# A layer norm's reciprocal deviation moved from GpSimd to ScalarE, with normalising and some partial sums one slot earlier

## The chip, the cores and the metric

The kernel runs on one core of one Trainium2 chip. The metric is the device time of one execution in microseconds (us), the median of three runs. All data are float32. A core has five engines that matter here: TensorE (PE in the profile; PEld is its weight load), VectorE (DVE), ScalarE (ACT), GpSimd (POOL) and SyncE (SP), which starts the transfers.

## The reference

Two layers work on x of shape (2, 256, 256, 128), each as x + f(group_norm(x)). The first is an attention along one image axis. The second, where the change lies, is a selective state-space scan:

```python
xz = x @ in_proj_w.T                      # 128 -> 2 x 256 channels
xi, z = jnp.split(xz, 2, axis=-1)
xi = silu(depthwise_conv3x3(xi) + conv_b)
xs = xi.reshape(B, 256, L)                # L = 256*256 positions in order
dts, Bs, Cs = split(x_proj_w @ xs)        # 8 + 16 + 16 rows
delta = softplus(dt_w @ dts + dt_b)
h = exp(delta*A) * h + (delta*xs) * Bs    # step by step along L, 16 states a channel
y = sum(h * Cs over states) + Ds * xs
mu = y.mean(-1); var = ((y - mu)**2).mean(-1)
y = (y - mu) * rsqrt(var + 1e-5) * ln_g + ln_b     # over the 256 channels
out = (y * silu(z)) @ out_proj_w.T
```

The change concerns the rsqrt in the layer norm, and the moments at which its result is used.

## The kernel before

The first part (lines up to about 560) makes weights and group statistics and runs the attention; it takes some 2670 us. The second part is one software pipeline over 128 **steps**. A step is four image rows of one image, T = 1024 positions. The 256 channels times 16 states are cut into **units** of 128 partitions: 32 channels times 4 states. So a step has 32 units; `unit(t)` splits slot number t into step k, channel half h, state group m and quarter q. The loop at the end of the kernel runs over **slots** t, one unit to a slot. Slots are counted here within their step, 0 to 31. Slot 0 of a step is the one in which its first unit is scanned.

What a unit goes through, each by one function:

- `decay` (L947, ScalarE): da = exp(a * delta), one slot ahead of the scan.
- `drive` (L957, GpSimd): hb = du * B for a pair of units, three slots ahead.
- `scan` (L969, VectorE): h = da*h + hb along the 1024 positions.
- `product` (L983, VectorE): yc = h * C. For the five pairs in `POOLED` (units 2-3, 6-7, 10-11, 18-19, 26-27) GpSimd makes it instead, as a pair, in `products` (L992). Both write into a pool with four yc buffers, each for a pair of units.
- `remember` (L974, ScalarE): keeps the last column of h as the next step's start. It is the last thing ScalarE does in a slot, so ScalarE follows VectorE slot by slot.
- `add_up` (L1014, TensorE): 16 matmuls that sum four units' yc over the states into the accumulator y. It is written at the end of slot u + 6 for the four units from u on, so in slots 2, 6, 10, ..., 30. A yc buffer is free only after it. With four buffers, the product of unit u + 8 needs those of u, and so waits for the sum of slot u + 6. For a group that opens a channel half it is preceded by `d_diag` (L1007), which starts y with Ds * xs.
- `y_out` (L1027, ScalarE): y to SBUF after the last sum of a half, in slots 4 and 20.

Two other strands are laid into the same slots by a table written by hand (`at(t, piece)`):

- `project` works about two steps ahead: `turn` and `normalise` (L652, L657), `conv` (L670; nine taps for each of four pieces, in slots 3 to 6, 11 to 14, 19 to 22 and 27 to 30), `conv_out` (L681), `gate` (L695, with `gate_out` L706), `states` (L718, L731), `size` (L736) with `size_out` (L747). All of these share one PSUM bank (`ps_p`, one buffer): the next matmul of this strand starts only when ScalarE has evacuated the one before. Silu and softplus (L689, L711, L755) follow, one big ScalarE operation each. [...] each has an ACT_TABLE_LOAD of its own, and the next exp (L947) has one to come back.
- `finish` works one step behind, on one row at a time. A row starts in slots 0, 8, 16 and 24. Its pieces and their offsets from there: `turn` 0 (L819, TensorE transposes and centres y), `stats` 1 (L831, ScalarE squares and sums), `scales` 2 (L838 and L839, GpSimd: variance, then power -0.5), `norm` 4 (L843, ScalarE), `back` 5 (L854, TensorE), `gated` 6 (L862, VectorE), `mix` 7 (L866, L870, TensorE: output sums), `leave` 8 (L880, ScalarE: to SBUF and out).

Within a slot the order is fixed: drive and products, decay, scan and product, `y_out`, then the pieces of the table with those of `finish` ahead of those of `project` and those that run on TensorE last, then `add_up`, then `remember`. Each engine takes its instructions in exactly that order.

Of the kernel before, what the change touches and what calls it, by code (L numbers as in the profile page):

```python
# [15 lines left out]
P = 128  # L16
# [5 lines left out]
def attn_then_ssm_kernel(  # L22
# [59 lines left out]
    make_identity(nc, ident)  # L82
    ones_mean = const0.tile([P, P], F32, name="ones_mean")
    nc.vector.memset(ones_mean, 1.0 / P)
    neg_half = const.tile([P, TB // P], F32, name="neg_half")
    nc.vector.memset(neg_half, -0.5)

# [188 lines left out]
    with ExitStack() as actx:  # L276
# [51 lines left out]
        def project(n, tag, name, w):  # L328
            o = calls[n]
            o[name + "_ps"] = bank(tag, f"{name}_ps", [P, TB])  # L330
            nc.tensor.matmul(o[name + "_ps"], w, o["xnc"], start=True, stop=True)
# [280 lines left out]
    nc.gpsimd.memset(xn, 0.0)  # L612
    given = {}

    def project(k):

        b, s = steps[k]
# [69 lines left out]

        def silu_xs():
            nc.scalar.activation(o["xs"], o["xs"], AF.Silu)  # L689
            v["xs"] = dr.tile([NH, P, T], F32, name="xs_d")  # L690
            nc.sync.dma_start(out=v["xs"].rearrange("h p t -> p h t"), in_=o["xs"])

# [16 lines left out]

        def silu_z():  # L710
            nc.scalar.activation(o["sz"], o["sz"], AF.Silu)  # L711
            v["sz"] = dr.tile([NH, P, T], F32, name="sz_d")
            nc.sync.dma_start(out=v["sz"].rearrange("h p t -> p h t"), in_=o["sz"])

# [38 lines left out]

        def softplus():
            nc.scalar.activation(o["delta"], o["delta"], AF.Softplus)  # L755
            v["delta"] = dr.tile([NH, P, T], F32, name="delta_d")
            nc.sync.dma_start(out=v["delta"].rearrange("h p t -> p h t"), in_=o["delta"])

# [43 lines left out]
    def finish_row(k, b, row, t0, a):  # L802
        o = {}

        def fetch():
            o["xres"] = s1.tile([P, WT, C], F32, name="xres")
            nc.sync.dma_start(
                out=o["xres"], in_=x1[b][row].rearrange("(t p) c -> p t c", p=P)
            )
            o["szr"] = s1.tile([P, NH, W], F32, name="szr")  # L810
            nc.sync.dma_start(
                out=o["szr"], in_=given[k]["sz"][:, :, t0 : t0 + W].rearrange("h p t -> p h t")
            )

        def turn():
            o["yt"] = ps_f.tile([P, WT, DI], F32, name="yt", tag="f")
            for j in range(WT):
                for h in range(NH):
                    nc.tensor.matmul(  # L819
                        o["yt"][:, j, :],  # L820
                        ys[k, h][:, t0 + j * P : t0 + (j + 1) * P],
                        centre[:, (1 - h) * P : (1 - h) * P + DI],
                        start=(h == 0),
                        stop=(h == NH - 1),
                    )

        def stats():
            yn = o["yn"] = s1.tile([P, WT, DI], F32, name="yn")
            o["ss"] = s2.tile([P, WT], F32, name="lss")
            for j in range(WT):  # L830
                nc.scalar.activation(  # L831
                    yn[:, j, :], o["yt"][:, j, :], AF.Square, accum_out=o["ss"][:, j : j + 1]
                )

        def scales():
            o["rstd"] = s2.tile([P, WT], F32, name="rstd")
            ve = s2.tile([P, WT], F32, name="lve")
            nc.gpsimd.tensor_scalar(ve, o["ss"], 1.0 / DI, LN_EPS, ALU.mult, ALU.add)  # L838
            nc.gpsimd.tensor_tensor(o["rstd"], ve, neg_half[:, 0:WT], ALU.pow)  # L839

        def norm():
            for j in range(WT):
                nc.scalar.activation(  # L843
                    o["yn"][:, j, :],
                    o["yt"][:, j, :],
                    AF.Copy,
                    scale=o["rstd"][:, j : j + 1],
                )

        def back():  # L850
            o["yd"] = ps_f.tile([P, NH, W], F32, name="yd", tag="f")
            for h in range(NH):
                for j in range(WT):
                    nc.tensor.transpose(  # L854
                        o["yd"][:, h, j * P : (j + 1) * P],
                        o["yn"][:, j, h * P : (h + 1) * P],
                        ident,
                    )

        def gated():  # L860
            o["yg"] = s1.tile([P, NH, W], F32, name="yg")
            nc.vector.tensor_tensor(o["yg"], o["yd"], o["szr"], ALU.mult)  # L862

        def mix():
            o["o"] = ps_f.tile([P, WT, C], F32, name="o1_ps", tag="f")
            nc.tensor.matmul(o["o"], ident, o["xres"], start=True, stop=False)  # L866
            for j in range(WT):
                for h in range(NH):
                    for i, by in enumerate(("yg", "szr")):
                        nc.tensor.matmul(  # L870
                            o["o"][:, j, :],
                            o[by][:, h, j * P : (j + 1) * P],
                            w_out[:, i, h, :],
                            start=False,
                            stop=(j == WT - 1 and h == NH - 1 and i == 1),
                        )

        def leave():
            ob = s1.tile([P, WT, C], F32, name="ob")
            nc.scalar.copy(ob, o["o"])  # L880
            nc.sync.dma_start(
                out=out_tok[b, row * W : (row + 1) * W, :].rearrange("(t p) c -> p t c", p=P),
                in_=ob,
            )

        at(a, fetch)
        for i, piece in (
            (0, turn),
            (1, stats),
            (2, scales),  # L890
            (4, norm),
            (5, back),
            (6, gated),
            (7, mix),
            (8, leave),
        ):
            at(a + i, piece, pe=piece in (turn, back, mix))
# [5 lines left out]
    def unit(t):  # L903

        k, i = divmod(t, NU)
        h, i = divmod(i, NM)
        m, q = divmod(i, NQ)
        return k, h, m, q
# [89 lines left out]
    def add_up(t):  # L998

        k, h, m, _ = unit(t)  # L1000
        if m == 0:
            xr = s1.tile([P, T], F32, name="xr")
            nc.sync.dma_start(out=xr, in_=given[k]["xs"][h])
            y = outs["y"] = ps_y.tile([P, T], F32, name="y")
            for i in range(NB):
                cols = slice(i * TB, (i + 1) * TB)
                nc.tensor.matmul(  # L1007
                    y[:, cols], d_diag[:, h, :], xr[:, cols], start=True, stop=False
                )
        y = outs["y"]  # L1010
        for i in range(NB):
            cols = slice(i * TB, (i + 1) * TB)
            for q in range(NQ):
                nc.tensor.matmul(  # L1014
                    y[q * CQ : (q + 1) * CQ, cols],
                    sel,
                    units[t + q]["yc"][:, cols],
                    start=False,
                    stop=(m == NSG - 1),
                )  # L1020
        for q in range(NQ):
            del units[t + q]

    def y_out(t):
        k, h, _, _ = unit(t)
        ys[k, h] = s2.tile([P, T], F32, name=f"ys{h}")
        nc.scalar.copy(ys[k, h], outs["y"])  # L1027
# [12 lines left out]
    with tc.manual_schedule(engines=engines):  # L1040
        for t in range(min(slots), max(slots) + 1):
            if 0 <= t + AHEAD < end:
                fetch(t + AHEAD)
            if 0 <= t < end and t % (NU * NSTEP) == 0:
                st = s1.tile([P, NCG, NSG], F32, name="state")
                nc.gpsimd.memset(st, 0.0)
                states_of[steps[t // NU][0]] = st
            if 0 <= t + 3 < end and t % 2:
                drive(t + 3)
            if 0 <= t - 2 < end and t % 2 == 0 and pooled(t - 2):  # L1050
                products(t - 2)
            if 0 <= t + 1 < end:
                decay(t + 1)
            if 0 <= t < end:
                scan(t)
                if not pooled(t):
                    product(t)
            if 0 <= t - 8 < end and unit(t - 8)[2:] == (NSG - 1, 0):
                y_out(t - 8)
            for pieces in slots.pop(t, ()):  # L1060
                for piece, args in pieces:
                    piece(*args)
            if 0 <= t - 6 < end and (t - 6) % NQ == 0:
                add_up(t - 6)
            if 0 <= t < end:
                remember(t)

# [36 lines left out]
```

## Time and profile before

16220.56 us, median of three runs (16212.09 to 16221.96).

| engine | busy, us | share of the span |
|---|---|---|
| VectorE | 14617.8 | 90% |
| TensorE | 14005.8 | 86% |
| GpSimd | 13488.7 | 83% |
| ScalarE | 10627.5 | 66% |

The costliest rows of the profile and what they are in the code:

| row | engine | number | mean ns |
|---|---|---|---|
| L957 drive | GpSimd | 2048 | 4542 |
| L992 products | GpSimd | 640 | 4542 |
| L969 scan | VectorE | 4096 | 2346 and 2335 |
| L983 product | VectorE | 2816 | 1225 |
| L947 decay | ScalarE | 4096 | 1117 |
| L1014 sums of y | TensorE | 16384 | 752 |
| L838, L839 scales | GpSimd | 512 each | 191 and 689 |
| L843 normalising | ScalarE | 1024 | 470 |

How to read what follows. A group line has the line number, engine, operation, output and inputs, shapes and count, then busy time and mean; after the second bar stands the idle time of the engine just before these instructions and what ended it. A line of a timeline has its start in us, its length, then the same names, and in brackets the idle time before it with the releaser. A line of a table by stretches has, after the stretch and its length, the busy time and count of PE, PEld, DVE, ACT and POOL, then the granted TensorE clock (1.00 is full), the busy share of the DMA engines and GB/s. A line of waits has the waiting instruction, what released it, the total in us, how many times and the longest.

### The profile page before, as it was taken

Reading aid. Unit: us, or ns where it says so; the run is one execution under the profiler, and the core shown is the slowest. Engines: PE = TensorE matmul, PEld = TensorE weight load, DVE = VectorE, ACT = ScalarE, POOL = GpSimd, SP = SyncE. Lnnn points to the kernel's source line nnn. Section 1 sums busy time; section 2 is a strip of 40 time slices with the busy share of each in tenths; the row PEclk is TensorE's granted clock in tenths of the full one; section 3 lists DMA queues with packets and bytes.
Section 4 is the critical chain, followed back from the end, with each engine's and each line's share of the span. In section 5 each row is a group of like instructions: output and inputs, shape, how many; then the busy total and the mean of one; then the engine's idle time right before and its main releaser. Section 6 shows DMA issues by size and latency. Waiting matters only on the chain. (4 is left out here: it accounts for less than half of the span.)

```text
span 16220.2 us, 178642 instructions
## 1 busy us (share of the span) xinstructions
PE 14005.8 (86%) x59451; PEld 7034.3 (43%) x59451; DVE 14617.8 (90%) x12483; ACT 10627.5 (66%) x18973; POOL 13488.7 (83%) x4240
## 2 busy tenths in 40 slices
PE   6999997888888888888888888888888888888886
PEld 5877883333333333333333333333333333333333
DVE  7665555999999999999999999999999999999998
ACT  3555554666666666666666666666666666666665
POOL 1111114999999999999999999999999999999998
PEclk8999998999999999999999889999999999999998
DMA  4322223666666666666666666666666666666665
GB/s 184 129 95 79 94 79 133 236 235 242 233 234 236 237 236 236 242 234 231 238 235 237 233 234 230 238 235 234 241 233 231 238 234 238 237 240 236 228 239 180
DMA packets 1428911, 3452.16 MB, mean 213 GB/s; under 512 B 119784, under 2 KB 711184, under 8 KB 1407504
## 3 DMA queue, kind: packets, MB, share of 16 engines
q1 hardware_dynamic: 1427984, 3440.73, 59.0%
q8 instruction: 468, 7.67, 0.2%
q14 instruction: 459, 3.76, 0.1%
HBM read 2752.41 MB, written 687.88 MB: 212 GB/s over the span
## 5 line engine op out<-in xcount | busy, mean ns | idle before, releaser
L957 POOL TENSOR_TENSOR hb<-du_r,bb 128x2048 f32<-128x2048 f32 x2048 | 9266.3, 4542 | 71.3 <-DMA du_r<-du_d 15.4
L969 DVE TENSOR_TENSOR_SCAN da<-da,state,hb 128x1024 f32<-128x1024 f32 x2816 | 6607.3, 2346 | 164.7 <-ACT da L947 131.5
L947 ACT ACTIVATE da<-delta_r,a_neg 128x1024 f32<-128x1024 f32 x4096 | 4575.5, 1117 | 84.2 <-DMA delta_r<-delta_d 0.2
L670 PE MATMUL u_ps<-xn,w_tap 128*128 128x512 f32 x9216 | 4230.8, 604 | 7.3 <-ACT sz L706 3.4
L983 DVE TENSOR_TENSOR yc<-da,cc 128x1024 f32<-128x1024 f32 x2816 | 3449.3, 1225 | 423.5 <-PE y L1014 257.4
L969 DVE TENSOR_TENSOR_SCAN hb<-da,state,hb 128x1024 f32<-128x1024 f32 x1280 | 2946.7, 2335 | 15.9 <-ACT da L947 15.9
L992 POOL TENSOR_TENSOR yc<-hb,cc 128x2048 f32<-128x2048 f32 x640 | 2906.7, 4542 | 62.3 <-ACT delta L747 46.8
L670 PEld LDWEIGHTS u_ps<-xn,w_tap 128*128 128x128 f32 x9216 | 1699.1, 194 | 2438.7 <-issue 2003.2
L1014 PE MATMUL y<-yc,sel 128*32 128x512 f32 x16384 | 2562.2, 752 | 14.8 <-POOL yc L992 14.8
L974 ACT COPY state<-da 128x1 f32<-128x1 f32 x2816 | 441.3, 157 | 2838.3 <-DVE yc L983 2797.8
L433 POOL TENSOR_TENSOR x1g<-xc,bo_all 128x512 f32<-128x512 f32 x256 | 315.7, 1272 | 1841.1 <-DVE stats L482 1839.2
L819 PE MATMUL yt<-centre,ys 128*128 128x256 f32 x4096 | 1037.6, 397 | 510.0 <-ACT ob L880 510.0
L695 PE MATMUL z_ps<-xn,w_z 128*128 128x512 f32 x1024 | 801.3, 875 | 696.1 <-ACT sz L706 424.0
L1014 PEld LDWEIGHTS y<-yc,sel 128*32 128x32 f32 x16384 | 492.5, 126 | 1942.6 <-issue 1703.9
L383 ACT ACTIVATE e<-s_ps,nmx 128x256 f32<-128x256 f32 x1024 | 477.0, 475 | 968.6 <-DVE nmx L374 939.9
L819 PEld LDWEIGHTS yt<-centre,ys 128*128 128x128 f32 x4096 | 744.6, 192 | 691.1 <-ACT ob L880 607.6
L736 PE MATMUL dt_ps<-xd,w_dt 8*128 8x512 f32 x1024 | 691.0, 759 | 350.9 <-ACT delta L747 233.2
L870 PE MATMUL o_ps<-w_out,szr 128*128 128x128 f32 x4096 | 797.7, 277 | 0.0
L870 PE MATMUL o_ps<-w_out,yg 128*128 128x128 f32 x4096 | 796.6, 276 | 0.0
L350 DVE TENSOR_TENSOR v<-v_ps,bv_all 128x512 f32<-128x512 f32 x256 | 177.0, 692 | 591.5 <-PE v_ps L343 591.5
L764 POOL TENSOR_TENSOR xs<-delta,xs 128x1024 f32<-128x1024 f32 x256 | 598.7, 2364 | 98.3 <-ACT delta L755 98.3
L870 PEld LDWEIGHTS o_ps<-w_out,yg 128*128 128x128 f32 x4096 | 666.9, 193 | 27.1
(132 smaller groups left out, 16764.6 us busy)
## 6 DMA issues: line engine op xcount, KB each, us to landing
bb<-bc_d SPq DMA_DIRECT2D x1024, 512.0 KB, 4.3
cc<-bc_d SPq DMA_DIRECT2D x1024, 512.0 KB, 4.4
delta_r<-delta_d SPq DMA_DIRECT2D x1024, 512.0 KB, 6.2
du_r<-du_d SPq DMA_DIRECT2D x1024, 512.0 KB, 6.1
sz_d<-sz SPq DMA_DIRECT2D x128, 1024.0 KB, 6.7
szr<-sz_d SPq DMA_DIRECT2D x512, 256.0 KB, 5.6
xs_d<-xs SPq DMA_DIRECT2D x128, 1024.0 KB, 6.6
xr<-xs_d SPq DMA_DIRECT2D x256, 512.0 KB, 5.0
```

What stands on the lines that cost most here:

```text
L670: nc.tensor.matmul(o["u"], w_tap[:, h, tap, :], xn[:, i * RB + dy : i * RB + dy + RB, dx : dx + W], start=(tap == 0), stop=(tap == 8),)
L695: nc.tensor.matmul(o["z"], w_z[:, h, :], xn[:, 1 + i * RB : 1 + (i + 1) * RB, 1 : W + 1], start=True, stop=True,)
L736: nc.tensor.matmul(o["dt"], w_dt[:, h, :], o["xd"][0:DR, i * TB : (i + 1) * TB], start=True, stop=True,)
L764: nc.gpsimd.tensor_tensor(du, o["delta"][:, h, :], du, ALU.mult)
L819: nc.tensor.matmul(o["yt"][:, j, :], ys[k, h][:, t0 + j * P : t0 + (j + 1) * P], centre[:, (1 - h) * P : (1 - h) * P + DI], start=(h == 0) ...
L870: nc.tensor.matmul(o["o"][:, j, :], o[by][:, h, j * P : (j + 1) * P], w_out[:, i, h, :], start=False, stop=(j == WT - 1 and h == NH - 1 an ...
L947: nc.scalar.activation(da, spreads["delta", k, h, q], AF.Exp, scale=a_neg[:, g, m : m + 1])
L957: nc.gpsimd.tensor_tensor(hb, spreads["pair", k, h, q], repeats["bb", k, h, m].unsqueeze(1).to_broadcast([P, 2, T]), ALU.mult,)
L969: nc.vector.tensor_tensor_scan(u["h"], u["da"], u["hb"], st, ALU.mult, ALU.add)
L983: nc.vector.tensor_tensor(u["yc"], u["h"], repeats["cc", k, h, m], ALU.mult)
L992: nc.gpsimd.tensor_tensor(yc, hb, repeats["cc", k, h, m].unsqueeze(1).to_broadcast([P, 2, T]), ALU.mult)
L1014: nc.tensor.matmul(y[q * CQ : (q + 1) * CQ, cols], sel, units[t + q]["yc"][:, cols], start=False, stop=(m == NSG - 1),)
```

## The change

The reciprocal deviation is made by two small ScalarE operations, rstd = exp(-0.5 * ln(ss/256 + eps)), in place of two on GpSimd. [...] Since rstd is then made on the engine that uses it, `norm` and `back` move one slot up (offsets 3 and 4). The sums of y for groups of four whose last unit is not in `POOLED` move one slot up as well, from u + 6 to u + 5: those of slots 2, 18 and 26 go to slots 1, 17 and 25. The other five, those of slots 6, 10, 14, 22 and 30, stay. `y_out` moves from slots 4 and 20 to 3 and 19.

```diff
+    ln_eps = const.tile([P, 1], F32, name="ln_eps")
+    nc.vector.memset(ln_eps, LN_EPS)
...
+    def exp_and_ln():
+        nc.scalar.preload_act_table_set("natural_log_exp_and_others")
...
             nc.scalar.activation(o["xs"], o["xs"], AF.Silu)
+            exp_and_ln()
...
             nc.scalar.activation(o["sz"], o["sz"], AF.Silu)
+            exp_and_ln()
...
             nc.scalar.activation(o["delta"], o["delta"], AF.Softplus)
+            exp_and_ln()
...
         def scales():
+            lv = s2.tile([P, WT], F32, name="lve")
+            nc.scalar.activation(lv, o["ss"], AF.Ln, bias=ln_eps, scale=1.0 / DI)
             o["rstd"] = s2.tile([P, WT], F32, name="rstd")
-            ve = s2.tile([P, WT], F32, name="lve")
-            nc.gpsimd.tensor_scalar(ve, o["ss"], 1.0 / DI, LN_EPS, ALU.mult, ALU.add)
-            nc.gpsimd.tensor_tensor(o["rstd"], ve, neg_half[:, 0:WT], ALU.pow)
+            nc.scalar.activation(o["rstd"], lv, AF.Exp, scale=-0.5)
...
-            (4, norm),
-            (5, back),
+            (3, norm),
+            (4, back),
...
-            if 0 <= t - 8 < end and unit(t - 8)[2:] == (NSG - 1, 0):
-                y_out(t - 8)
+            if 0 <= t - 7 < end and unit(t - 7)[2:] == (NSG - 1, 0):
+                y_out(t - 7)
...
-            if 0 <= t - 6 < end and (t - 6) % NQ == 0:
-                add_up(t - 6)
+            for u in (t - 6, t - 5):
+                if 0 <= u < end and u % NQ == 0 and (u == t - 6) == pooled(u + NQ - 1):
+                    add_up(u)
```

## The prediction, made before the changed kernel was run

> **What bounds the kernel now.** I read the engine table first, then the loop alone, VectorE's waits, and one step in order of time. The state-space loop runs from 2673 to about 16160 us: 128 steps of 32 slots, one scan per slot.
>
> ```profile
> PE 14005.8 (86%) x59451; PEld 7034.3 (43%) x59451; DVE 14617.8 (90%) x12483; ACT 10627.5 (66%) x18973; POOL 13488.7 (83%) x4240
> ```
> ```profile
> 3092.00:15745.00 12653.00, 10890.65 (x43200) 4813.22 (x43200) 12205.01 (x6960) 8663.23 (x14400) 12345.80 (x3724) 0.91 0.66 236
> ```
> ```profile
> DVE yc L983 <- PE y L1014: 246.6, 285, 2.0
> DVE da L969 <- POOL hb L957: 28.0, 94, 1.0
> ```
>
> The second line is 120 steps of 105.44 us. POOL is busiest (12345.8, 98%), VectorE next (96%), yet VectorE hardly waits for POOL (28 us): POOL keeps just ahead. Of VectorE's 448 us of idle time some 400 sit before its product, and the named part, 246.6 us or 2.06 us a step, is for a yc buffer that TensorE's sums must free. So VectorE's own work is the floor and late sums are what lies above it. Where, the step whose slot 0 starts at 6879.53 shows, on VectorE, TensorE and ScalarE:
>
> ```profile
> 6918.18 1.23 DVE L983 TENSOR_TENSOR yc<-da,cc 128x1024 f32<-128x1024 f32 x1 [0.93 <-PE y L1014]
> 6945.34 1.23 DVE L983 TENSOR_TENSOR yc<-da,cc 128x1024 f32<-128x1024 f32 x1 [0.51 <-PE y L1014]
> 6972.69 1.22 DVE L983 TENSOR_TENSOR yc<-da,cc 128x1024 f32<-128x1024 f32 x1 [1.02 <-PE y L1014]
> ```
> ```profile
> 6888.63 1.12 PE L736 MATMUL dt_ps<-xd,w_dt 8*128 8x512 f32 x2 [0.86 <-ACT xd L731]
> 6889.68 1.92 PE L1014 MATMUL y<-yc,sel 128*32 128x512 f32 x16
> 6891.54 5.42 PE L670 MATMUL u_ps<-xn,w_tap 128*128 128x512 f32 x12
> ...
> 6912.50 2.07 PE L736 MATMUL dt_ps<-xd,w_dt 8*128 8x512 f32 x2 [1.14 <-ACT delta L747]
> 6914.50 3.64 PE L1014 MATMUL y<-yc,sel 128*32 128x512 f32 x16
> ```
> ```profile
> 6890.16 0.67 ACT L747 ACTIVATE delta<-dt_ps,dtb_c 128x512 f32<-128x512 f32 x1
> ...
> 6892.41 1.00 ACT L1027 COPY ys<-y 128x1024 f32<-128x1024 f32 x1
> 6893.31 0.83 ACT L843 ACTIVATE yn<-yt,rstd 128x256 f32<-128x256 f32 x2
> ```
>
> The three waits are in slots 12, 20 and 28; each product needs the buffers of the sum that stands in slot 10, 18 or 26. That sum takes 3.64 us there and 1.92 in slot 2: after small matmuls with gaps between them TensorE runs at half speed.
>
> [...] the same 16 matmuls take 1.92 or 3.64 us, and the granted clock between 6912 and 6918.5 is 0.51. [...]
>
> **The change, part by part.**
>
> *Off POOL.* Two operations a row (191 and 689 ns), four rows a step: 3.5 us of 105 off POOL, with its wait for row statistics (132.1 us in the loop). It removes the 28 us wait for hb, 0.23 us a step, and in the tail, where POOL's step stands in the chain, about 1.2 us for each of four rows.
>
> *Table loads.* Three functions a step leave exp's set, so three loads back; before, they stood ahead of the next exp (360 in 120 steps), now ahead of the state copy. Equal count, in slots where ScalarE then waits for the scan anyway: nothing.
>
> *Ln and Exp on ScalarE,* 128x2 each, unseen in this trace. Below: the column copy L974, 157 ns, so 0.3 us the pair. [...] I take 0.4. Behind them in slots 2, 10, 18 and 26 stands the evacuation (xd, delta, sz, xn) that frees the one projection bank. In slot 10 TensorE waits for exactly that (1.14 us, "ACT delta"), and its half-speed sum is what VectorE's slot 12 waits for: 0.4 us on the path.
>
> *Sums up a slot.* Of eight sums a step, five end in a POOL pair and stay: that of slot 10 stays. Those of slots 2, 18 and 26 move to 1, 17 and 25. In 17 and 25 they fill gaps of 1.68 and 2.14 us that stand before half-speed matmuls, so they start some 3.7 and 4.1 us sooner, right behind the second z_ps (ends 6937.98) and t_ps (6964.87), and at full speed. Slots 20 and 28 stop waiting: 0.51 + 1.02 us here. As a share of the three waits that is 1.53 of 2.46, so on average 2.06 x 0.62 = 1.28; with hb's 0.23 **1.5 us a step gained**.
>
> *Slots 3 and 19: what the move costs.* y's copy (1.00) and the normalising (0.83) come from slots 4 and 20 to 3 and 19, and the change's order puts both ahead of that slot's evacuation. In slot 3: scales in slot 2 delay xd by 0.4, but decay of slot 4 still starts near 6889.2 and ends at 6890.2; copy to 6891.2, normalising to 6892.0, then delta's evacuation to 6892.6. The convolution needs the bank, and starts at 6892.6, not 6891.54: **1.05 us late**, with all its work still to do. From there TensorE runs without a gap through the output sums that end at 6905.95, for which ScalarE waits 1.34 us in slot 8, and then into the chain of slots 8 to 10. So the delay reaches slot 12.
>
> *The clock in slot 3.* The sum is now before dt_ps, so dt_ps (8 rows) is followed by an idle gap: sum to 6889.7, dt_ps to 6890.75, idle to 6892.6. That is 2.9 us of almost no work. [...] slots 17 to 18 have 1.66 us idle plus part of 1.68 and go slow, slots 1 to 2 (1.98 us, half of it dt_ps) mostly don't. [...]
>
> *How much reaches VectorE.* The trace has a step in which the matmuls just before were slow:
>
> ```profile
> 6461.90 3.17 PE L718 MATMUL xd_ps<-xs,w_xp 128*64 128x512 f32 x4
> ```
> ```profile
> 6497.51 1.23 DVE L983 TENSOR_TENSOR yc<-da,cc 128x1024 f32<-128x1024 f32 x1 [1.79 <-PE y L1014]
> ```
>
> Its convolution starts 13.46 us into the step (6471.24 - 6457.78), not 12.01: 1.45 late. Slot 12's product starts 39.73 in, not 38.65: 1.08 late. So three quarters arrive.
>
> *Sum.* Loss 0.75 x (1.05 + 1.5) + 0.4 = 2.3; gain 1.5; net +0.8 us a step, x 128 = +102, tail -5: **16,318, say 16,320 us** (+0.6%). The convolution of slot 19 has the same delayed evacuation, but its sum has gone ahead: it starts 1.6 us earlier at best, and lost clock gives that back. ScalarE has a 0.8 us margin there for the next exp. I cost it at nothing.
>
> **The rivals.**
> - *Faster: slot 3 keeps its clock.* Loss 0.75 x 1.05 + 0.4 = 1.2, or 0.8 if Ln and Exp hide: -0.3 to -0.7 us a step, 16,180 to 16,130; middle 16,150. For it: [...] the gain is a wait plainly named. Against it: 2.9 us in one stretch is longer than what loses the clock elsewhere.
> - *No change: gain and loss cancel,* with slow windows in half the steps: 0.75 x (1.05 + 0.7) + 0.4 = 1.7 against 1.5, within 30 us: 16,230.
> - *Slower still: two slow windows in most steps.* 0.75 x 3.95 + 0.4 = 3.4 against 1.5: +1.9 x 128, 16,460. For it: TensorE also reaches slot 31 earlier and idles longer before slot 0, and the step shown above lost its clock right there. [...]
>
> A POOL bound is no rival: it gets 3.5 us lighter.
>
> **How the numbers follow.** Forecast 0.47, faster 0.27, no change 0.13, slower still 0.13. The range leaves out part of the two ends: 16,130 holds nearly all of the faster case, 16,440 stops short of the last. Faster 0.27, same 0.13, slower 0.60.
>
> **What the changed profile would show.** Right: VectorE's waits for the sums vanish in slots 20 and 28 and grow in slot 12 from 0.9 to some 2 us or more; the convolution of slot 3 starts about 13 us into a step, often at half clock; POOL never holds a scan; table loads stay at six a step; Ln plus Exp near 0.4 us. Wrong, if that convolution starts at 12.0 or keeps its clock: then the faster case holds. It would also be wrong if new waits of VectorE for exp showed in the short slots 10, 11, 18 and 19: ScalarE late, slower than forecast.

## The result and the profile after

After: 16317.17 us, median of four runs (16311.47 to 16327.24). Before, beside it: 16221.26 us (16212.09 to 16227.36). The ratio is 1.006, with a 95% interval of 1.0043 to 1.0078: the change costs some 96 us. The forecast was 16,320 us, slower.

The engine table of the changed kernel, and the 120 steps that the prediction took as a stretch of before:

```profile
PE 13759.1 (84%) x59451; PEld 7060.9 (43%) x59451; DVE 14627.3 (90%) x12484; ACT 10765.8 (66%) x20003; POOL 13051.0 (80%) x3216
```
```profile
3089.15:15835.38 12746.23, 10654.40 (x43200) 4839.01 (x43200) 12214.31 (x6961) 8783.51 (x15360) 11936.23 (x2764) 0.94 0.68 234
```

GpSimd lost 1024 instructions in all and 410 us in the stretch, as asked of it. TensorE even shows 236 us less busy time, and its granted clock rises from 0.91 to 0.94: on the whole the change loses less clock than before, so where it is lost has to matter. VectorE's own work is the same (12214 against 12205 us), yet a step takes 106.22 us against 105.44. So VectorE idles more, and the profile has to say where. The groups of ScalarE, drive on GpSimd, and VectorE's two largest sums of waits in the same stretch:

```profile
L619 ACT ACT_TABLE_LOAD x360 | 461.9, 1283 | 6.5
L846 ACT ACTIVATE lve<-lss,ln_eps 128x2 f32<-128x2 f32 x480 | 134.3, 280 | 0.0
L848 ACT ACTIVATE rstd<-lve 128x2 f32<-128x2 f32 x480 | 97.7, 203 | 15.2
```
```profile
L966 POOL TENSOR_TENSOR hb<-du_r,bb 128x2048 f32<-128x2048 f32 x1921 | 8685.9, 4546 | 476.3 <-DVE da L978 429.3
```
```profile
DVE yc L992 <- PE y L1023: 265.2, 221, 2.2
DVE hb L978 <- ACT da L956: 109.7, 122, 11.3
```

The changed program makes its own loads behind each silu and softplus (L619): 360, three a step, of 1283 ns each. Before, as many stood ahead of the next exp:

```profile
L947 ACT ACT_TABLE_LOAD x360 | 461.9, 1283 | 6.4
```

After, no load stands ahead of Ln, Exp or the exp of `decay`: the other 360 are those of silu and softplus (L695, L718, L763; 120 each). Ln takes 280 ns, Exp 203 ns. GpSimd now waits for VectorE, and VectorE no longer waits for hb (28.0 us before). Its waits for sums have grown a little (246.6 us before), those for exp from 15.3 us to 109.7.

The time of a slot, from the start of its scan to the start of the next one, averaged over the loop, shows where steps lengthen. Since a scan that waits starts late, its wait counts to the slot before. Only slots that moved are listed:

| slot | before, us | after, us | difference |
|---|---|---|---|
| 8 | 3.57 | 4.08 | +0.51 |
| 10 | 2.27 | 3.15 | +0.89 |
| 11 | 2.25 | 2.33 | +0.08 |
| 12 | 4.39 | 5.11 | +0.72 |
| 19 | 2.57 | 2.24 | -0.33 |
| 20 | 3.89 | 3.57 | -0.33 |
| 28 | 4.34 | 3.57 | -0.78 |

The last three give 1.44 us, the first four take 2.20; the slots not listed hardly move. By releaser, VectorE's waits in the 120 steps are: at the product of slot 8, for its sum, 70.2 us in 101 steps (before: none); at the scan of slot 11, for exp, 96.4 us in all 120 (before: none); at the product of slot 12, for its sum, 195.0 us (before: 109.3). One step, whose slot 0 starts at 6905.66, shows what stands behind each. First VectorE: the product of slot 8, the scan of slot 11, and the products of slots 12, 20 and 28:

```profile
6932.39 1.23 DVE L992 TENSOR_TENSOR yc<-da,cc 128x1024 f32<-128x1024 f32 x1 [0.61 <-PE y L1023]
...
6940.24 2.35 DVE L978 TENSOR_TENSOR_SCAN hb<-da,state,hb 128x1024 f32<-128x1024 f32 x1 [0.82 <-ACT da L956]
...
6946.85 1.23 DVE L992 TENSOR_TENSOR yc<-da,cc 128x1024 f32<-128x1024 f32 x1 [1.81 <-PE y L1023]
...
6973.26 1.23 DVE L992 TENSOR_TENSOR yc<-da,cc 128x1024 f32<-128x1024 f32 x1
...
6999.67 1.23 DVE L992 TENSOR_TENSOR yc<-da,cc 128x1024 f32<-128x1024 f32 x1
```

The brackets of slots 20 and 28 are empty: those waits are gone. Two waits for sums of y remain, and a scan that waits for exp is new. The same step on TensorE:

```profile
6913.83 1.92 PE L1023 MATMUL y<-yc,sel 128*32 128x512 f32 x16
6915.68 1.12 PE L744 MATMUL dt_ps<-xd,w_dt 8*128 8x512 f32 x2
6918.66 4.54 PE L676 MATMUL u_ps<-xn,w_tap 128*128 128x512 f32 x6 [1.86 <-ACT delta L755]
...
6934.39 0.39 PE L879 MATMUL o_ps<-w_out,szr 128*128 128x128 f32 x2
...
6941.55 2.07 PE L744 MATMUL dt_ps<-xd,w_dt 8*128 8x512 f32 x2 [0.78 <-ACT delta L755]
6943.55 3.25 PE L1023 MATMUL y<-yc,sel 128*32 128x512 f32 x16
```

And on ScalarE, in slots 2 and 3, and then in slot 8:

```profile
6914.13 0.28 ACT L846 ACTIVATE lve<-lss,ln_eps 128x2 f32<-128x2 f32 x1
6914.44 0.20 ACT L848 ACTIVATE rstd<-lve 128x2 f32<-128x2 f32 x1
6914.56 0.56 ACT L739 COPY xd<-xd_ps 64x512 f32<-64x512 f32 x1
...
6916.29 1.00 ACT L1036 COPY ys<-y 128x1024 f32<-128x1024 f32 x1
6917.20 0.83 ACT L852 ACTIVATE yn<-yt,rstd 128x256 f32<-128x256 f32 x2
6917.91 0.69 ACT L755 ACTIVATE delta<-dt_ps,dtb_c 128x512 f32<-128x512 f32 x1
...
6934.81 0.37 ACT L889 COPY ob<-o_ps 128x256 f32<-128x256 f32 x1 [4.03 <-PE o_ps L879]
```

Read the three together. In slot 3 the copy of y (1.00) and the normalising (0.83) stand ahead of the 0.69 us that empties the one projection bank. TensorE waits 1.86 us for it, after dt_ps, and starts the convolution 13.0 us into the step. Its first six matmuls then take 4.54 us; an undisturbed dozen takes 5.42 (before's timeline, in the prediction). The stretch from 6918.50 to 6922.00 has a granted clock of 0.57. From here all is later: output sums end at 6934.78, 29.1 us into the step (26.4 in the step shown of before; on average over 120 steps 29.1 against 26.6), so ScalarE waits 4.03 us in slot 8 to take them out, and its exp, which stands behind, reaches the scan of slot 11 late (0.82 us, in slot 10's time). The sum for slot 8's product is late on TensorE itself: the 101 steps in which that product waits are exactly the 101 of 120 in which the first six matmuls of the convolution run slow (4.1 to 4.5 us; 2.8 in the others).

### The profile page after: what moved, and what is told of

It is laid out like the page before. It is cut to its first block, busy times and chain, and to the rows that moved or that the text cites. A ratio compares the mean times of both kernels' runs of the same rounds, so it can differ in the third digit from the quotient of the medians.

```text
span 16309.7 us, 178677 instructions
## 1 busy us (share of the span) xinstructions
PE 13759.1 (84%) x59451; PEld 7060.9 (43%) x59451; DVE 14627.3 (90%) x12484; ACT 10765.8 (66%) x20003; POOL 13051.0 (80%) x3216
## 5 line engine op out<-in xcount | busy, mean ns | idle before, releaser
L676 PE MATMUL u_ps<-xn,w_tap 128*128 128x512 f32 x9216 | 4537.7, 641 | 657.4 <-ACT sz L713 433.7
L676 PEld LDWEIGHTS u_ps<-xn,w_tap 128*128 128x128 f32 x9216 | 1792.6, 204 | 3099.4 <-issue 2065.9
L1023 PE MATMUL y<-yc,sel 128*32 128x512 f32 x16384 | 2192.7, 654 | 18.1 <-POOL yc L1001 18.1
L1023 PEld LDWEIGHTS y<-yc,sel 128*32 128x32 f32 x16384 | 452.6, 115 | 1499.1 <-issue 1318.1
L702 PE MATMUL z_ps<-xn,w_z 128*128 128x512 f32 x1024 | 568.2, 636 | 332.3 <-ACT sz L713 241.2
```

Of the source, the lines that this page charges most:

```text
L676: nc.tensor.matmul(o["u"], w_tap[:, h, tap, :], xn[:, i * RB + dy : i * RB + dy + RB, dx : dx + W], start=(tap == 0), stop=(tap == 8),)
L702: nc.tensor.matmul(o["z"], w_z[:, h, :], xn[:, 1 + i * RB : 1 + (i + 1) * RB, 1 : W + 1], start=True, stop=True,)
L1023: nc.tensor.matmul(y[q * CQ : (q + 1) * CQ, cols], sel, units[t + q]["yc"][:, cols], start=False, stop=(m == NSG - 1),)
```

## The experiments

The first theory was the prediction's: the order in slot 3 costs about 2 us a step through a late evacuation and a lost clock, while Ln and Exp cost little. Rivals: Ln and Exp themselves carry the loss, or the sums' new places do. In the table "against before" is the difference of the medians of one comparison, "a step" is the mean over the 120 steps of the profile.

| kernel | median, us | ratio (95%) | against before | a step |
|---|---|---|---|---|
| before | 16211.75 to 16221.26 | 1 | 0 | 105.44 |
| after | 16317.17 | 1.006 (1.0043 to 1.0078) | +96 | 106.22 |
| Ln and Exp alone | 16432.23 | 1.0132 (1.0118 to 1.0145) | +215 | 107.18 |
| moves alone | 16191.37 | 0.9983 (0.9977 to 0.999) | -26 | 105.20 |
| Ln and Exp alone, behind the evacuation | 16192.77 | 0.9987 (0.998 to 0.9994) | -19 | 105.22 |
| after, all small work behind | 16106.00 | 0.993 (0.9917 to 0.9942) | -111 | 104.48 |
| after, only Ln and Exp behind | 16290.41 | 1.0047 (1.0034 to 1.0059) | +79 | 105.98 |
| after, only copy and normalising behind | 16143.07 | 0.9957 (0.9945 to 0.9969) | -69 | 104.82 |
| after, a matmul added in slot 2 | 16257.46 | 1.0022 (1.0013 to 1.0032) | +40 | 105.76 |
| after, `leave` first | 16286.92 | 1.0042 (1.0029 to 1.0055) | +68 | 105.96 |
| after, `leave` first, a matmul added | 16169.26 | 0.9968 (0.9955 to 0.998) | -50 | 105.02 |
| all behind, sum of slot 10 in slot 9 | 16077.37 | 0.9916 (0.9902 to 0.993) | -134 | 104.24 |
| the same, `leave` first | 15991.58 | 0.9859 (0.9845 to 0.9872) | -228 | 103.58 |

### Ln and Exp alone

The changed kernel with its moves taken back, so that of the change only the two operations and the table loads are left.

```diff
-            (3, norm),
-            (4, back),
+            (4, norm),
+            (5, back),
...
-            if 0 <= t - 7 < end and unit(t - 7)[2:] == (NSG - 1, 0):
-                y_out(t - 7)
+            if 0 <= t - 8 < end and unit(t - 8)[2:] == (NSG - 1, 0):
+                y_out(t - 8)
...
-            for u in (t - 6, t - 5):
-                if 0 <= u < end and u % NQ == 0 and (u == t - 6) == pooled(u + NQ - 1):
-                    add_up(u)
+            if 0 <= t - 6 < end and (t - 6) % NQ == 0:
+                add_up(t - 6)
```

> The kernel before with Ln and Exp on ScalarE and the table set loaded by the program; normalising, sums and y's copy stay where they were. Theory (the moves into slot 3 are the cost): POOL's 3.5 us a step are gone, worth 0.23 us a step, and Ln with Exp (0.48 us in the changed kernel's trace) delays slot 10's evacuation by 0.4, so 105.6 us a step and 16,220 to 16,250 us. Rival (Ln and Exp on ScalarE are the cost): most of the loss is here, 16,290 us or more.

Measured 16432.23 us, +215: slower than the whole change, and the worst miss of the study. TensorE in slots 1 to 3 of the step that starts at 6956.98:

```profile
6966.49 1.12 PE L744 MATMUL dt_ps<-xd,w_dt 8*128 8x512 f32 x2 [1.27 <-ACT xd L739]
6967.54 3.58 PE L1023 MATMUL y<-yc,sel 128*32 128x512 f32 x16
6971.06 5.42 PE L676 MATMUL u_ps<-xn,w_tap 128*128 128x512 f32 x12
```

Before, the same three lines (in the prediction) had a gap of 0.86 us, a sum of 1.92 and a convolution 12.0 us into the step. Ln and Exp stand ahead of xd's evacuation and push it 0.42 us; the gap grows to 1.27, and with the 1.12 us of dt_ps behind it, matmuls over 8 rows only, that is enough to lose the clock: in 119 of 120 steps the sum takes longer than 1.92 us. Here it takes 3.58, and the convolution starts 14.1 us in (13.7 on average). From there the delay goes on to VectorE as in the changed kernel: the slot-to-slot times of slots 10, 12 and 20 grow by 0.75, 1.09 and 0.16 us against before.

### The moves alone

The kernel before with the sums and the copy of y in their new places; `pow` stays on GpSimd and normalising in its old slot.

```diff
-            if 0 <= t - 8 < end and unit(t - 8)[2:] == (NSG - 1, 0):
-                y_out(t - 8)
+            if 0 <= t - 7 < end and unit(t - 7)[2:] == (NSG - 1, 0):
+                y_out(t - 7)
...
-            if 0 <= t - 6 < end and (t - 6) % NQ == 0:
-                add_up(t - 6)
+            for u in (t - 6, t - 5):
+                if 0 <= u < end and u % NQ == 0 and (u == t - 6) == pooled(u + NQ - 1):
+                    add_up(u)
```

> The kernel before with the three sums and y's copy one slot earlier, nothing else: power stays on GpSimd, normalising in its old slot. Theory: slots 20 and 28 stop waiting (1.28 us a step); the copy alone delays slot 3's evacuation, the convolution starts 0.35 us late instead of 1.05 and loses its clock in about half of the steps, so about 0.2 us a step gained, 16,160 to 16,220 us. Rival (Ln and Exp are the cost): all of the gain stays, 16,050 us. Rival (a sum ahead of slot 2's small matmul is the cost by itself): as slow as the changed kernel, 16,310 us.

Measured 16191.37 us, -26, as expected, though only in part by the expected way: 29 of 120 steps lose the clock in slot 3, but 62 lose it before slot 0 (11 in the kernel before), of which the expectation said nothing. So the parts do not add: +215 and -26 make +189, but together they cost 96. The early sum spares the added operations part of their price. The timelines show how: with the sum in slot 1, TensorE has it to do while xd is on its way, 1.92 us at full clock in all 120 steps of the changed kernel; with Ln and Exp alone it waits idle, and the sum behind takes 3.58.

### Ln and Exp alone, behind the evacuation

The kernel with Ln and Exp alone, the pieces of a slot sorted so that `scales` comes after what else ScalarE has in it.

```diff
-            for pieces in slots.pop(t, ()):
-                for piece, args in pieces:
-                    piece(*args)
+            act, pe = slots.pop(t, ((), ()))
+            late = [p for p in act if p[0].__name__ in ("scales",)]
+            for piece, args in [p for p in act if p not in late]:
+                piece(*args)
+            for piece, args in (*late, *pe):
+                piece(*args)
```

> Ln and Exp alone, as in the run that came out at 16,432 us, but behind the slot's evacuation of the projection bank instead of ahead of it. Theory (their place in ScalarE's queue costs, and through it TensorE's clock in slot 2; the 0.48 us of work itself is hidden): the convolution of slot 3 starts at 12.0 us into the step again, and POOL's relief stays: 16,170 to 16,215 us. Rival (the work itself, or the answer coming later than GpSimd gave it, costs): 16,350 us or more.

Measured 16192.77 us, as expected: 234 us come back from order alone (+215 against -19), with the same instructions. The convolution of slot 3 starts 12.0 us into the step again. So not the half microsecond on ScalarE costs 215 us, but the delay of the evacuation behind it.

### After, with small work behind the evacuations

Three kernels, the same sorting in the changed kernel: all small work (`late` has `scales` and `norm`, and y's copy stands behind the evacuations too), only `scales`, and only `norm` with y's copy.

```diff
+            act, pe = slots.pop(t, ((), ()))
+            late = [p for p in act if p[0].__name__ in ("scales", "norm")]
+            for piece, args in [p for p in act if p not in late]:
+                piece(*args)
             if 0 <= t - 7 < end and unit(t - 7)[2:] == (NSG - 1, 0):
                 y_out(t - 7)
-            for pieces in slots.pop(t, ()):
-                for piece, args in pieces:
-                    piece(*args)
+            for piece, args in (*late, *pe):
+                piece(*args)
```

All:

> The changed kernel with one thing else: within a slot ScalarE evacuates the projection bank first, then copies y, then does Ln and Exp or the normalising. Same work, same slots. Theory (the evacuation behind them is the cost): the convolution of slot 3 starts near 11.9 us into the step, full clock, the whole gain of 1.5 us a step stays: 16,020 to 16,060 us. Rivals (ScalarE's added work, or the sum's place in slot 1): 16,290 us or more.

Only `scales`:

> The changed kernel with Ln and Exp behind the slot's evacuation; y's copy and the normalising stay ahead of it. Theory now: in slot 2 the early sum already covers Ln and Exp, so only slot 10 gains its 0.4 us, and the convolution of slot 3 still starts at 13.0: 16,240 to 16,290 us. Rival (Ln and Exp ahead are the whole loss, since alone they cost 215 us): 16,110 us, as with all three behind.

Only `norm` and y's copy:

> The changed kernel with y's copy and the normalising behind the slot's evacuation; Ln and Exp stay ahead of it. Theory (slot 3 is where the changed kernel loses): the convolution starts at 11.9 us into the step at full clock, slot 10 keeps its 0.4 us: 16,110 to 16,165 us. Rival (Ln and Exp ahead are the whole loss): 16,300 us as the changed kernel.

Measured 16106.00, 16290.41 and 16143.07 us. Against after's +96 that is -207, -17 and -165 us. Copy and normalising ahead of the evacuation are the cost inside the changed kernel; Ln and Exp ahead of it are worth little there (the intervals of +96 and +79 overlap; the step is 0.24 us shorter). The sorting acts in every slot that has such work, not in slot 3 alone, but what it brings back shows in slots 8 to 12, just behind slot 3. The convolution of slot 3, copy and normalising behind, in the step from 6963.33, one of those that lose the clock before slot 0:

```profile
6965.11 2.91 PE L828 MATMUL yt<-centre,ys 128*128 128x256 f32 x8 [2.68 <-ACT ob L889]
...
6976.89 2.84 PE L676 MATMUL u_ps<-xn,w_tap 128*128 128x512 f32 x6 [0.78 <-ACT delta L755]
```

The wait for delta falls from 1.86 to 0.78 us and six matmuls from 4.54 to 2.84, even here. The second and third kernel came out as expected, but for the third the expected start of the convolution, 11.9 us in, holds in only 39 of 120 steps. The kernel with all behind missed its 16,020 to 16,060. What keeps both from more is in the first line: a new idle time of 2.68 us before slot 0, since TensorE runs ahead and then waits for ScalarE to take out the output sums of the row before (`leave`). In more than half of the steps (69 of 120 with all behind, 80 in this one) the clock is lost there: the eight matmuls take 2.91 us here instead of 2.00, and the convolution starts 13.6 us in; in the others 11.9.

### A matmul added in slot 2

The changed kernel with one matmul more, 128 rows, whose result lands in dt's bank and is overwritten by the next one. It does nothing but fill TensorE's idle time.

```diff
+            if (h, i) == (0, 0):
+                nc.tensor.matmul(
+                    o["dt"], w_z[:, h, :], o["xs"][:, h, i * TB : (i + 1) * TB],
+                    start=True, stop=True,
+                )
```

> The changed kernel with one more 128x512 matmul a step: in slot 2, into the bank that the step-size matmul then overwrites, so the output is the same. It fills the time in which TensorE idles anyway, and shortens the stretch of almost no work from 2.9 to some 1.9 us. Theory (half clock after that stretch is half of the loss): the convolution still starts at 13.0 but at full speed, output sums end near 27.6 instead of 29.1 us into the step, 16,160 to 16,220 us. Rival (the clock plays no part, only the late start): added work changes nothing or slows, 16,310 us or more.

Measured 16257.46 us: -56 against after, less than expected. Where the clock was kept at slot 0 most steps fell to 103.7 to 104.8 us, but in 59 of 120 it was lost there, as above. So the question was put again with that spot mended in both kernels: `leave` of slot 0 goes ahead of the exp in its slot.

```diff
+            here = slots.get(t, ((), ()))[0]
+            for p in [p for p in here if p[0].__name__ == "leave" and t % NU == 0]:
+                here.remove(p)
+                p[0]()
             if 0 <= t + 1 < end:
                 decay(t + 1)
```

With `leave` first, without the matmul:

> The changed kernel with only the copy of slot 0 ahead of exp, the control for the filled run. Theory: slot 3 still loses its clock in three steps of four, so output sums still end near 29.1 us into the step: 16,270 to 16,320 us. Rival (slot 0 is where the clock matters): as fast as the filled run.

With both:

> The changed kernel with both idle stretches of TensorE in slots 0 and 2 kept short: the copy ahead of exp in slot 0, and the filling matmul in slot 2. Late evacuation in slot 3 and Ln and Exp ahead in slot 10 are unchanged. Theory (half clock makes up most of the changed kernel's loss): convolution at 13.0 us into the step in all steps, at full clock, output sums end at 27.4, as the steps of the filled run that kept their clock (103.7 to 104.8 us): 16,060 to 16,130 us, below the kernel before. Rival (the late start itself is most of the loss): 16,250 us or more.

Measured 16286.92 and 16169.26 us: the added matmul makes the kernel 118 us faster, 0.94 us a step. Without it, in the step from 6908.80, and with it, in the step from 6866.75:

```profile
6921.79 4.49 PE L676 MATMUL u_ps<-xn,w_tap 128*128 128x512 f32 x6 [1.88 <-ACT delta L755]
...
6937.47 0.39 PE L879 MATMUL o_ps<-w_out,szr 128*128 128x128 f32 x2
```
```profile
6876.75 1.12 PE L745 MATMUL dt_ps<-xs,w_z 128*128 128x512 f32 x2
6877.81 1.12 PE L749 MATMUL dt_ps<-xd,w_dt 8*128 8x512 f32 x2
6879.75 2.84 PE L676 MATMUL u_ps<-xn,w_tap 128*128 128x512 f32 x6 [0.82 <-ACT delta L760]
...
6893.78 0.39 PE L884 MATMUL o_ps<-w_out,szr 128*128 128x128 f32 x2
```

Both start the convolution 13.0 us in; the evacuation is late in both. With the matmul it runs at full clock and the output sums end 27.4 instead of 29.1 us into the step. Slot 8 goes from 4.04 to 3.69 us and slot 10 from 3.10 to 2.48, but slot 12 stays (4.99 and 5.07). So the half clock of slot 3 is what slots 8 and 10 pay; slot 12's share is not due to it. The filled kernel says the same within itself: 28 of its 120 steps still lose the clock in slot 3, and they take 105.88 us on average, the others 104.76. The expected 16,060 to 16,130 assumed that none would; 28 of 120 at 1.1 us are some 33 us over 128 steps by my estimate, most of the miss.

### One more early sum, and `leave` first

The kernel with all small work behind, and the sum of slot 10, for which slot 12's product waits, made in slot 9:

```diff
             for u in (t - 6, t - 5):
-                if 0 <= u < end and u % NQ == 0 and (u == t - 6) == pooled(u + NQ - 1):
+                late = pooled(u + NQ - 1) and u % NU != 4
+                if 0 <= u < end and u % NQ == 0 and (u == t - 6) == late:
                     add_up(u)
```

> The version with all evacuations first (16,106 us), and the sum of slot 10 one slot earlier too, in the gap of slot 9. Its POOL pair is ready by then (done 30 us into the step, the gap begins near 31). Theory: the wait of slot 12 goes, 0.6 to 0.9 us a step, and with it the half clock in slots 10 to 12: 15,980 to 16,050 us, faster than all so far. Rival (the next thing takes its place, TensorE waiting for POOL in slot 9): 16,100 us or more.

Measured 16077.37 us, only 23 to 29 below the kernel it is made from and above what was expected. VectorE's waits for sums were gone, but waits for exp had come in their place (107.3 us, 178 times, in the 120 steps); in 60 steps the clock is lost before slot 0, and slots 3 and 4 are longer. With `leave` of slot 0 ahead of exp (the edit above) on top:

> The fastest version so far (16,077 us) with one 0.37 us copy 1.05 us earlier: in slot 0 ScalarE takes the output sums of the row before out of their bank ahead of exp, not behind it. TensorE then idles 1.6 instead of 2.7 us before the sums of slot 0. Theory (the half clock that half of the steps have in slots 0 to 2 is what is left): all steps start their convolution at 11.9 us, some 0.9 us a step less, 15,940 to 15,990 us. Rival (the idle time there is not what costs, another wait takes its place): 16,060 us or more.

Measured 15991.58 us, 2 us above the expected range, the fastest of the study and 1.4% below before (ratio 0.9859, 0.9845 to 0.9872). The step from 6809.07 on TensorE, and VectorE's two largest sums of waits in 12430 us of loop (us in all, number, longest):

```profile
6809.68 2.00 PE L828 MATMUL yt<-centre,ys 128*128 128x256 f32 x8 [1.51 <-ACT ob L889]
...
6820.96 2.84 PE L676 MATMUL u_ps<-xn,w_tap 128*128 128x512 f32 x6 [0.78 <-ACT delta L755]
```
```profile
DVE da L978 <- ACT da L956: 21.7, 29, 1.6
DVE hb L978 <- ACT da L956: 15.2, 2, 13.1
```

The idle time before slot 0 is 1.51 instead of 2.68 us, the eight matmuls take 2.00 instead of 2.91, and VectorE's busy time in the stretch is 12205 us of 12430, 98%. What is left is nearly all VectorE's own work; of the 15.2 us, 13.1 are one single wait.

## Why the prediction was right

*Off GpSimd, and the table loads:* as forecast. GpSimd lost 3.4 us a step (3.5 said) and never held a scan; the loads number 360 in 120 steps and cost nothing visible.

*Ln and Exp, 0.4 us:* my estimate, above the 0.3 of two column copies. The pair takes 0.28 + 0.20 us and pushes xd's evacuation by 0.42. But the term in the sum, 0.4 us a step through slot 10, was about twice too large: putting them behind brings 0.24 us a step in the changed kernel. And it was no property of the pair: in the old order the same 0.42 us costs 215 us, which the working could not have told, since it added the parts' prices.

*Gain of 1.5 us a step:* 1.44 measured. Slot 28 gave 0.78 and slot 20 0.33, in sum 1.11 against 1.28. Slot 19 gave 0.33, and that is GpSimd's relief (0.23 said): both kernels with Ln and Exp alone give it too (2.57 to 2.24 us), the moves alone do not, and all 28.0 us for which VectorE waited for hb before stood at the scan of slot 20.

*Late start of slot 3:* the convolution starts 13.0 us in, as forecast, in 89 of 120 steps (mean 13.3). That the small work ahead of delta's evacuation does it is shown by moving it behind: 0.78 instead of 1.86 us of wait, and -165 us.

*Lost clock in slot 3:* the 1.5 us a step for it in the sum was my estimate, and so were the 0.7 and 2.9 us in its place in the rivals "no change" and "slower still"; the trace of before did not show them. In the changed kernel 101 of 120 steps lose it there. That the lost clock costs by itself is shown by the added matmul: 0.94 us a step with the start unmoved, where the prediction's term was 0.75 x 1.5 = 1.1, 0.75 being the share of a delay that arrives.

*Lost clock before slot 0:* the sum put this at nothing; the prediction named it only for the slower rival. It came in 29 steps of 120 (11 before), in which the convolution starts about 14.2 us in. With `leave` first, which is meant for just this, no step has it any more (ten more lose the clock in slot 3 instead), and a step takes 105.96 us, not 106.22; the intervals of the two kernels overlap.

*How it reaches VectorE:* here a step failed. "So the delay reaches slot 12", in three quarters, was the claim, with slot 12's wait growing "from 0.9 to some 2 us or more". Of 2.20 us lost only 0.72 is in slot 12. Slot 8 has 0.51, where the sum of slot 6 is late behind the half-speed convolution; slots 10 and 11 have 0.97, where exp for the next scan is late because ScalarE waits 4.03 us for the output sums in slot 8. The prediction saw that wait at 1.34 us and did not ask what stands behind it: exp. It also said that waits for exp in slots 10 and 11 would mean a slower result than forecast; they came (109.7 us in the 120 steps; before, VectorE waited 15.3), and the result was as forecast, since the three places together make the 2.2 us where it had put 2.3 into one. The size of the delay was right: on average the output sums end 2.6 us later than before, as the 1.05 + 1.5 of the working. That the forecast came within 3 us of the measured time is luck: Ln and Exp were put too large, the clock before slot 0 at nothing, and the share of the delay that arrives was taken from one step, for a way that carries only a third of it.

*Slot 19 at nothing:* held; slots 19 to 22 show no loss.

Open: which share of slot 12's 0.72 us comes from the late start alone. No kernel here moves only that; Ln and Exp behind the evacuation take 0.28 of it away (slot 12 at 4.82 us, not 5.11). Open, too, is why the steps of after alternate between about 105.3 and 106.4 us. What differs in them is seen: in all 57 steps near 106.4 the last dt_ps of slot 10, which stands ahead of the sum for slot 12, takes 2.07 us, in all 37 near 105.3 it takes 1.12.

## What to carry to other kernels

On an engine that takes its instructions in order, what empties a buffer another engine waits for goes first, and small side work behind it: in this kernel the order alone was worth 165 to 234 us where it mattered. Ask of each move how long it leaves TensorE idle between small matmuls, not only who waits for it: the clock lost in slot 3 was paid in slots 8 and 10 (0.35 and 0.62 us). And don't add prices of parts that were taken alone: here +215 and -26 made +96.

## What the runs showed of the hardware

- A gap of 1.27 instead of 0.86 us before two 8-row matmuls (1.12 us) was the difference between 3.58 and 1.92 us for the 16 matmuls behind them.
- With 1.88 us idle behind two 8-row matmuls, the first six matmuls of the convolution took 4.49 us; with the added matmul ahead of those two and 0.82 us idle, 2.84 us (the two kernels with `leave` first). In the step of the changed kernel shown, the granted clock is 1.00 from 6913.83 to 6915.70 and 0.57 from 6918.50 to 6922.00. How much idle time it takes to lose the clock, these runs do not settle.
- An added matmul, 1.12 us a step of work for nothing, made the kernel 118 us faster (16286.92 to 16169.26).
- Ln, with its bias from the tile `ln_eps`, took 280 ns on 128x2, and Exp, with none, 203. After a load of 1283 ns the next operation started 11 to 12 ns later.
